# Final sums of batches 1 to 4 beside the expert blocks, with a check of the counts on the chip and a branch that repeats them

## The chip, the core and the metric

The kernel runs on one core of one Trainium2 chip. TensorE (PE in the profile; PEld is its weight load) multiplies matrices, VectorE (DVE) and ScalarE (ACT) work elementwise, GpSimd (POOL) issues here the indirect DMAs, and SyncE (SP) issues plain ones. Each engine runs its own instruction stream in order; semaphores tie them together. The metric is the device time of one execution in microseconds (us), as a median of runs. The kernel before took 1891.41 us (three runs, 1890.63 to 1898.66).

## What is computed

Eight batches of 512 tokens with 256 features (4096 tokens in all) go through four residual steps:

```python
x = x + attn_a(layernorm(x), ...)   # projection, silu, a recurrence with decay 0.9, projection
x = x + ffn(layernorm(x), ...)      # mixture of experts
x = x + attn_b(layernorm(x), ...)   # causal attention, 16 heads of 16
x = x + ffn(layernorm(x), ...)      # the mixture once more, same weights
```

The mixture picks 4 of 16 experts for each token (two of four groups, then the best four in them), runs a gated network of width 256 in each picked expert, weights the four results, and adds a shared network that every token passes:

```python
topk_idx, tw = _route(x, router_w, bias)
routed = sum over the picked experts e of  tw[e] * ((silu(x @ gate_w[e]) * (x @ up_w[e])) @ down_w[e])
sh = silu(x @ sh_gate_w) * (x @ sh_up_w) @ sh_down_w
return routed + sh
```

## The kernel before, in words

The work has two pairs of stages: a stretch over the eight batches (first the recurrence, then the attention), and after each stretch a routed stage, in which the picked experts run. Weights of all experts stay in on-chip memory (`w_all`).

*In a stretch*, batch by batch, the tokens are normalised and routed. `choices` finds each token's four experts and its place among the rows of each expert: `row` is a running count of the rows of each expert, carried from batch to batch in `counts[i]` (L610 to L613), so after batch b it says how many rows each of the 16 experts has up to there, plus the fixed start of the expert's region. One indirect DMA of GpSimd per 128 tokens and choice (L648) writes the normalised tokens, their weights and their token numbers into `xg`, sorted by expert. `shared_experts` computes the shared network. Two arrays in device memory, `parts[i][0]` and `parts[i][1]`, hold the result of the mixture in two halves: the residual rows are stored into the first (`part<-x`), the shared network's into the second (`part<-ys_m`), and what the experts make is later added into both.

`blocks` (L662) then makes a table of blocks. A block is 128 rows of one expert. The order of the blocks is by their number within an expert first and by expert second: the first block of all experts, then the second of all that have one, and so on. Since rows are sorted in the order of batches, early batches lie in early blocks. The number of blocks of each expert is `nb`. There are at most 143 blocks (`NBLK`), and 136 (`LIKELY`) are always run.

*In a routed stage* (`routed`, L748), a block n passes five steps: `load` (SP reads the 128 rows from `xg`), `fetch` (ACT and DVE copy the expert's gate and up weights to a fixed place, L787), `turn` (PE transposes the rows, L794, ACT copies them, L795), `up` (PE, sixteen matmuls, L805, then ACT and two DVE multiplications, L813 to L815), and `down` (PE, four matmuls, L833, ACT scales, L841). `down` ends with an indirect DMA of GpSimd, the scatter (L842), that adds the rows of the block into one of the two halves of `parts[i]`: even blocks into the first, odd ones into the second. `run` interleaves the steps of neighbouring blocks: the load is two blocks ahead of `up`, `fetch` and `turn` one ahead, `down` two behind. The tiles of the rows come from a set of nine buffers (tag `kb4`), so that a load for block n uses the buffer whose last reader was the scatter of block n-9. The copied weights share six buffers (tag `col`).

Ahead of the 136 blocks stands a branch (L875): all five engines load the number of blocks, compare it with 136, and take either an arm that runs blocks 136 to 142 or an arm that only brings the semaphores to the counts which the first one would have left.

`beside` is a dictionary from a block number to functions: after `down(n - 2)` the functions of key n - 1 are called. In the second routed stage it holds the final sums of batches 0 and 1. The final sum of a batch reads its rows of both halves of `parts[1]`, adds them on VectorE (L1289) and stores them to the output. `DONE` says after how many blocks a batch is complete whatever the routing: 64 for batch 0, 128 for batch 1, 143 for the others. So batch 0 is loaded at block 64 and added and stored at block 69, batch 1 at 128 and 133. These loads and stores are issued by GpSimd (L1282, L1292), into the buffers of `xpool` (three) and of the attention's values (two). The addition is pinned behind what was traced before it on VectorE. The other six batches are summed after the last block: SP loads one half, ACT the other, and they store in turn; their tiles use the nine `kb4` buffers.

The order of instructions on an engine is settled when the program is built, by a scheduler that works through the traced instructions by priority and readiness and places a semaphore wait wherever data, a buffer or an order in a DRAM tensor asks for one: a load from a half of `parts[1]` waits for all scatters into that half that come before it, and a scatter after it waits for the load. Scatters into the same half follow each other. The two arms of a branch are scheduled as a unit.

Of the kernel before, what the change touches and what calls it, by code (L numbers as in the profile page):

```python
# [10 lines left out]
FP = mybir.dt.float32  # L11
AF = mybir.ActivationFunctionType
ALU = mybir.AluOpType
AX = mybir.AxisListType

P = 128
B, T, D = 8, 512, 256
NT = T // P
# [8 lines left out]
E, F = 16, 256  # L27
# [19 lines left out]
NJ = NTOK // BLK  # L47
DONE = [min(E * (b + 1) * NT, NBLK) for b in range(B)]
CAND = NJ * E // P
WEXP = 2 * KD * F + KF * D  # L50
I32 = mybir.dt.int32
# [3 lines left out]
KB, COLS = 9, 6  # L55
HALVED = 1597463007.0
SENT = 8
EARLY = 2
PICKS = 5
ES, QK = 6, 6  # L60
ATT_SCALE = 0.25
# [9 lines left out]
def tile_hybrid_block(  # L71
# [22 lines left out]
    nc = tc.nc  # L94
# [3 lines left out]
    work = ctx.enter_context(tc.tile_pool(name="work", bufs=2))  # L98
    small = ctx.enter_context(tc.tile_pool(name="small", bufs=2))
# [86 lines left out]
    def load_expert(e: int):  # L186
# [13 lines left out]
        out=before,  # L200
        in_=before,
# [17 lines left out]
    def load_attention_weights():  # L219
# [16 lines left out]
        out=causal, in_=causal, compare_op=ALU.is_ge, fill=0.0, base=0, pattern=[[0, 2], [1, P]], channel_multiplier=-1  # L236
# [6 lines left out]
        out=tri, in_=tri, compare_op=ALU.is_gt, fill=0.0, base=0, pattern=[[1, P]], channel_multiplier=-1  # L243
# [6 lines left out]
    region = const.tile([P, E], FP, name="region")  # L250
# [252 lines left out]
        return sel  # L503

    counts = [region, region]

    class Route:

# [44 lines left out]
    def choices(i: int, b: int, tag: str, held):  # L553
# [57 lines left out]
        for t in range(NT):  # L611
            nc.vector.tensor_add(row[:, t + 1, :], pr[:, 1, t, :], row[:, t, :])
        counts[i] = row[:, NT, :]  # L613
        where = small.tile([P, NT, E], FP, tag="where", name=f"where_{tag}", bufs=1)
        nc.vector.tensor_add(where, pr[:, 0], row[:, 0:NT, :])
        yield
# [45 lines left out]
    def blocks(i: int, table):  # L662
# [67 lines left out]
        for which in range(2):  # L730
# [7 lines left out]
            else:  # L738
# [3 lines left out]
                    behind_all, number[0:1, :], total[0:1, :], float(E * REG), ALU.is_ge, ALU.mult  # L742
                )
                nc.vector.tensor_add(lines[:, 1, :], pl, behind_all)
        table += [lines[:, 0, :], lines[:, 1, :], expert, many]
        yield

    def routed(i: int, table, beside):  # L748

        weight_at, row_at, expert, many = table  # L750
        ACT, DVE = mybir.EngineType.Activation, mybir.EngineType.DVE
        PE, SP = mybir.EngineType.PE, mybir.EngineType.SP
        held = {}
# [520 lines left out]

    with banks_of(big=4, misc=2, y=2):

        def sum_of(b: int, homes):

            both = []
            for j, queue in enumerate((nc.sync, nc.scalar) if b >= EARLY else (nc.gpsimd, nc.gpsimd)):  # L1280
                both.append(homes(j))
                queue.dma_start(  # L1282
                    out=both[j],
                    in_=parts[1][j][b * T : (b + 1) * T, :].rearrange("(p t) d -> p (t d)", p=P),
                )
            return both

        def add_up(b: int, both):
            added = nc.vector.tensor_add(both[0], both[0], both[1])  # L1289
            if b < EARLY:  # L1290
                tc.keep_in_program_order(added)
            ((nc.sync, nc.scalar)[b % 2] if b >= EARLY else nc.gpsimd).dma_start(  # L1292
                out=out[b].rearrange("(p t) d -> p (t d)", p=P), in_=both[0]
            )

        sums = {}

        def early(b: int):
            def homes(j: int):
                tile = xpool.tile([P, NT, D], FP, tag="x", name=f"sum_{b}_0") if j == 0 else values(f"sum_{b}_1")  # L1300
                return tile.rearrange("p t d -> p (t d)") if j == 0 else tile[:, 0 : NT * D]

            return {
                DONE[b]: [lambda: sums.update({b: sum_of(b, homes)})],
                DONE[b] + 5: [lambda: add_up(b, sums.pop(b))],
            }

        routed(1, table, {**early(0), **early(1)})
        for b in range(EARLY, B):
            add_up(  # L1310
                b,
                sum_of(b, lambda j: work.tile([P, NT * D], FP, tag="kb4", name=f"sum_{b}_{j}", bufs=KB)),
            )


# [40 lines left out]
```

## Time and profile before

The profile is of one execution of 1906.2 us, with a span of 1904.0 us from the first to the last instruction and a mean granted TensorE clock of 0.945.

| | start us | end us |
|---|---|---|
| first routed stage, first to last transposes | 407.2 | 796 |
| second routed stage, first transposes on PE | 1471.5 | |
| last matmul of the stage | | 1865.0 |
| last scatter issued by GpSimd | 1872.7 | |
| first loads of the closing sums, SP and ACT | 1874.3 | 1876.6 |
| first and last closing addition | 1883.2 | 1900.1 |
| end of the span | | 1904.0 |

Over the span PE is busy 1723.5 us (91%), DVE 1085.4 (57%), ACT 797.3 (42%) and POOL 764.1 (40%). In the profile, a line of a timeline gives the start, the duration, the engine, the line of the kernel, the operation, the tiles it writes and reads, and in square brackets how long the engine was idle before it and what ended that wait. Neighbouring equal instructions are merged (x4), and the duration is then that of the whole group. A sequencer's own instructions carry a q (SPq, ACTq): their duration is that of issuing a DMA, not of the transfer.

### The profile page before, as it was taken

The numbers are of one execution on the slowest core, as the hardware profiler recorded it, in microseconds if no ns is written. First come the engines' busy times: TensorE is split into PE (matmuls) and PEld (weight loads), VectorE is DVE, ScalarE is ACT, GpSimd is POOL, SyncE is SP. The second block draws the span as 40 slices with busy tenths as digits, with TensorE's granted clock in tenths as the row PEclk, the third lists the DMA queues.
The fourth block names the chain that finished last, engine by engine and source line by source line (L and its number), as shares of the span: only waits on it lengthen the run. The fifth ranks groups of instructions, "written<-read, shape, count | busy, mean of one in ns | idle before, by whom it ended". The sixth has DMA issues, their size and how long they took to land. (4 is left out here: it accounts for less than half of the span.)

```text
span 1904.0 us, 32586 instructions
## 1 busy us (share of the span) xinstructions
PE 1723.5 (91%) x10640; PEld 1277.8 (67%) x10640; DVE 1085.4 (57%) x3378; ACT 797.3 (42%) x1628; POOL 764.1 (40%) x665
## 2 busy tenths in 40 slices
PE   5899999969999999899988989889886999999991
PEld 3566656559999999834444535445354999999991
DVE  6866666525555655657746556456543555555552
ACT  2322222125555555455534444344411555555550
POOL 4254544345555555500223031230333455565552
PEclk9899999889999999999989989899888999999996
DMA  4443321435555655511112111021144455565557
GB/s 157 155 140 122 125 75 72 145 105 95 96 98 103 106 96 96 93 39 34 41 40 81 45 48 57 36 86 45 65 146 138 80 96 97 95 130 95 96 101 240
DMA packets 149995, 181.35 MB, mean 95 GB/s; under 512 B 16096, under 2 KB 136960, under 8 KB 149824
## 3 DMA queue, kind: packets, MB, share of 16 engines
q0 software_dynamic: 53136, 76.81, 22.4%
q1 hardware_dynamic: 94320, 96.12, 16.6%
q10 hardware_dynamic: 2368, 6.29, 0.8%
q8 instruction: 89, 1.46, 0.3%
q14 instruction: 82, 0.67, 0.1%
HBM read 81.62 MB, written 97.53 MB: 94 GB/s over the span
## 5 line engine op out<-in xcount | busy, mean ns | idle before, releaser
L842 POOL DMA_INDIRECT part<-rows x272 | 425.9, 1566 | 367.9 <-ACT rows L841 317.5
L648 POOL DMA_INDIRECT xg<-sorted_m,slots_m x256 | 257.3, 1005 | 268.4 <-DVE sorted_m L638 133.8
L805 PEld LDWEIGHTS ph<-rows,gate 128*128 128x128 f32 x2176 | 285.8, 193 | 15.2 <-ACT rows L795 1.1
L805 PE MATMUL ph<-rows,gate 128*128 128x128 f32 x2176 | 289.0, 277 | 0.6 <-ACT rows L795 0.6
L805 PE MATMUL ph<-rows,up 128*128 128x128 f32 x2176 | 289.1, 277 | 0.0
L833 PE MATMUL pyr<-w_all,rows 128*128 x1088 | 282.1, 382 | 4.4 <-DVE rows L815 3.4
L805 PEld LDWEIGHTS ph<-rows,up 128*128 128x128 f32 x2176 | 266.5, 193 | 0.0
L813 ACT ACTIVATE rows<-ph 128x256 f32<-128x256 f32 x272 | 104.2, 383 | 330.2 <-PE ph L805 326.2
L814 DVE TENSOR_TENSOR rows<-ph,rows 128x256 f32<-128x256 f32 x272 | 115.4, 424 | 201.9 <-ACT rows L813 165.1
L833 PEld LDWEIGHTS pyr<-w_all,rows 128*128 128x128 f32 x1088 | 186.0, 192 | 19.0 <-issue 3.2
L787 ACT COPY gate<-w_all 128x512 f32 x272 | 170.0, 626 | 14.2 <-DVE up L787 2.0
L1039 ACT ACTIVATE w_all<-ps_a 128x1024 f32<-128x1024 f32 x128 | 124.8, 1021 | 111.6 <-PE ps_a L1028 63.6
L787 DVE COPY up<-w_all 128x512 f32 x272 | 117.9, 434 | 48.0 <-ACTq L875 25.2
L1028 PE MATMUL ps_a<-w_all 32*128 32x512 f32 (+3 forms) x1024 | 129.8, 488 | 15.0 <-issue 7.3
L922 PE MATMUL pd_m<-sd_sb,act_m 128*128 128x256 f32 x512 | 133.3, 409 | 5.4 <-DVE act_m L913 3.6
L841 ACT ACTIVATE rows<-pyr,gain 128x256 f32<-128x256 f32 x272 | 128.4, 472 | 20.1 <-PE pyr L833 18.6
L894 PE MATMUL pg_m<-xT_m,su_sb 128*128 128x512 f32 x256 | 132.0, 640 | 4.9 <-DVE x L426 3.9
L794 PE MATMUL pt<-ident,rows 128*128 128x128 f32 x544 | 105.0, 275 | 33.2 <-DMA rows<-xg 33.2
L894 PE MATMUL pg_m<-xT_m,sg_sb 128*128 128x512 f32 x256 | 127.4, 621 | 0.3 <-issue 0.3
L922 PEld LDWEIGHTS pd_m<-sd_sb,act_m 128*128 128x128 f32 x512 | 104.1, 207 | 30.5 <-issue 6.1
L815 DVE TENSOR_TENSOR rows<-ph,rows 128x256 f32<-128x256 f32 x272 | 115.2, 424 | 8.2
L818 DVE SCALAR_TENSOR_TENSOR gain<-rows,expert_b 128x4 f32<-128x4 f32 x272 | 60.4, 222 | 97.8 <-ACT rows L841 85.0
(207 smaller groups left out, 2199.6 us busy)
## 6 DMA issues: line engine op xcount, KB each, us to landing
rows<-xg SPq DMA_DIRECT2D x272, 136.0 KB
part<-x SPq DMA_DIRECT2D x16, 512.0 KB
part<-ys_m SPq DMA_DIRECT2D x16, 512.0 KB
w_all<-in_L_ffn_gate_w_dram SPq DMA_DIRECT2D x24, 256.0 KB
w_all<-in_L_ffn_up_w_dram SPq DMA_DIRECT2D x24, 256.0 KB
w_all<-in_L_ffn_down_w_dram SPq DMA_DIRECT2D x24, 256.0 KB
xg<-zeros SPq DMA_DIRECT2D x34, 136.0 KB
part<-rows POOLq DMA_INDIRECT x272
```

The source lines that it names most:

```text
L648: nc.gpsimd.indirect_dma_start(out=xg[i], out_offset=bass.IndirectOffsetOnAxis(ap=slots[:, at : at + 1], axis=0), in_=rows[:, t, :], in_of ...
L787: copy(here, w_all[:, bass.ds(held[n][0] + half * KD * F, KD * F)])
L805: nc.tensor.matmul(ph[:, s, f * P : (f + 1) * P], lhsT=both[s][:, k * F + f * P : k * F + (f + 1) * P], rhs=rows[:, ROW + k * P : ROW + (k ...
L814: nc.vector.tensor_mul(act, ph[:, 0, :], act)
L815: nc.vector.tensor_mul(act, ph[:, 1, :], act)
L833: nc.tensor.matmul(py, lhsT=act[:, f * P : (f + 1) * P], rhs=w_all[:, bass.ds(w + 2 * KD * F + f * D, D)], start=(f == 0), stop=(f == KF - 1),
L841: nc.scalar.mul(rows[:, 0:D], py, gain[:, TK : TK + 1])
L842: nc.gpsimd.indirect_dma_start(out=parts[i][n % 2], out_offset=bass.IndirectOffsetOnAxis(ap=rows[:, D + 2 * TK : D + 2 * TK + 1].bitcast(U ...
L894: nc.tensor.matmul(dst, lhsT=w[:, k, f * P : (f + 1) * P], rhs=xnT[:, k, :], start=(k == 0), stop=(k == KD - 1),)
L922: nc.tensor.matmul(py[:, j, :], lhsT=acts[n][:, f, t * P : (t + 1) * P], rhs=shared[n][3][:, f, :], start=(n == 0 and f == 0), stop=(n == ...
L1028: nc.tensor.matmul(ps[j // 2][:, j % 2, col : col + n], lhsT=k_sb[w][r, o, c * P : (c + 1) * P], rhs=q_sb[r, o, c * P : T], start=True, st ...
L1039: nc.scalar.activation(es[two], ps[two][:, :, 0:cols], AF.Exp, scale=ATT_SCALE)
```

## The change

The dictionary `SUMMED` takes the place of `EARLY` and `DONE` for the final sums: batches 0 to 4 are summed beside the blocks, loaded at blocks 64, 76, 88, 110 and 127 and added and stored five blocks later, all loads and stores issued by GpSimd. Only batches 5 to 7 are always summed after the last block.

Blocks 76, 88, 110 and 127 are not late enough for every possible routing. So `choices` keeps the counts after each of the batches 0 to 4 (`upto`), and `check`, beside blocks 14, 18, 22 and 26, works out from them how many blocks of the order the batch needs: the rows of each expert up to this batch, in blocks; the largest of these over the experts; the sum over the experts of the smaller of that and the expert's number of blocks. It marks the batch in `lates` if that is more than `SUMMED` allows. `checked`, beside block 40, adds up the marks. After the last block SP, ACT and VectorE load the sum of marks into registers; if it is above zero, a branch repeats the sums of batches 0 to 4.

```diff
--- before.py
+++ after.py
@@ -55,7 +55,9 @@
 KB, COLS = 9, 6
 HALVED = 1597463007.0
 SENT = 8
-EARLY = 2
+
+
+SUMMED = {0: DONE[0], 1: 76, 2: 88, 3: 110, 4: 127}
 PICKS = 5
 ES, QK = 6, 6
 ATT_SCALE = 0.25
@@ -503,6 +505,7 @@
         return sel
 
     counts = [region, region]
+    upto = {}
 
     class Route:
 
@@ -611,6 +614,9 @@
         for t in range(NT):
             nc.vector.tensor_add(row[:, t + 1, :], pr[:, 1, t, :], row[:, t, :])
         counts[i] = row[:, NT, :]
+        if i == 1 and b in SUMMED:
+            upto[b] = small.tile([1, E], FP, tag=f"upto_{b}", name=f"upto_{b}", bufs=1)
+            nc.vector.tensor_copy(upto[b], row[0:1, NT, :])
         where = small.tile([P, NT, E], FP, tag="where", name=f"where_{tag}", bufs=1)
         nc.vector.tensor_add(where, pr[:, 0], row[:, 0:NT, :])
         yield
@@ -742,12 +748,12 @@
                     behind_all, number[0:1, :], total[0:1, :], float(E * REG), ALU.is_ge, ALU.mult
                 )
                 nc.vector.tensor_add(lines[:, 1, :], pl, behind_all)
-        table += [lines[:, 0, :], lines[:, 1, :], expert, many]
+        table += [lines[:, 0, :], lines[:, 1, :], expert, many, nb]
         yield
 
     def routed(i: int, table, beside):
 
-        weight_at, row_at, expert, many = table
+        weight_at, row_at, expert, many, _ = table
         ACT, DVE = mybir.EngineType.Activation, mybir.EngineType.DVE
         PE, SP = mybir.EngineType.PE, mybir.EngineType.SP
         held = {}
@@ -1274,10 +1280,12 @@
 
     with banks_of(big=4, misc=2, y=2):
 
-        def sum_of(b: int, homes):
+        beside = (nc.gpsimd, nc.gpsimd)
+
+        def sum_of(b: int, homes, queues=(nc.sync, nc.scalar)):
 
             both = []
-            for j, queue in enumerate((nc.sync, nc.scalar) if b >= EARLY else (nc.gpsimd, nc.gpsimd)):
+            for j, queue in enumerate(queues):
                 both.append(homes(j))
                 queue.dma_start(
                     out=both[j],
@@ -1285,13 +1293,11 @@
                 )
             return both
 
-        def add_up(b: int, both):
+        def add_up(b: int, both, queues=(nc.sync, nc.scalar)):
             added = nc.vector.tensor_add(both[0], both[0], both[1])
-            if b < EARLY:
+            if queues is beside:
                 tc.keep_in_program_order(added)
-            ((nc.sync, nc.scalar)[b % 2] if b >= EARLY else nc.gpsimd).dma_start(
-                out=out[b].rearrange("(p t) d -> p (t d)", p=P), in_=both[0]
-            )
+            queues[b % 2].dma_start(out=out[b].rearrange("(p t) d -> p (t d)", p=P), in_=both[0])
 
         sums = {}
 
@@ -1301,16 +1307,62 @@
                 return tile.rearrange("p t d -> p (t d)") if j == 0 else tile[:, 0 : NT * D]
 
             return {
-                DONE[b]: [lambda: sums.update({b: sum_of(b, homes)})],
-                DONE[b] + 5: [lambda: add_up(b, sums.pop(b))],
+                SUMMED[b]: [lambda: sums.update({b: sum_of(b, homes, beside)})],
+                SUMMED[b] + 5: [lambda: add_up(b, sums.pop(b), beside)],
             }
 
-        routed(1, table, {**early(0), **early(1)})
-        for b in range(EARLY, B):
-            add_up(
-                b,
-                sum_of(b, lambda j: work.tile([P, NT * D], FP, tag="kb4", name=f"sum_{b}_{j}", bufs=KB)),
+        late = small.tile([1, 1], I32, tag="late", name="late", bufs=1)
+        lates = small.tile([1, len(SUMMED)], FP, tag="lates", name="lates", bufs=1)
+        nc.gpsimd.memset(lates, 0.0)
+
+        def check(b: int):
+
+
+            nb = table[4]
+            one = small.tile([1, E + 2], FP, tag="one", name=f"one_{b}", bufs=1)
+            n, most, done = one[:, 0:E], one[:, E : E + 1], one[:, E + 1 : E + 2]
+            nc.vector.tensor_sub(n, upto[b], region[0:1, :])
+            shape = [1, E, NJ]
+            more = work.tile(shape, FP, tag="col", name=f"above_{b}", bufs=COLS)
+            nc.vector.tensor_tensor(
+                more, n.unsqueeze(2).to_broadcast(shape), steps[0:1, :].unsqueeze(1).to_broadcast(shape), ALU.is_gt
             )
+            nc.vector.tensor_reduce(n, more, AX.X, ALU.add)
+            nc.vector.tensor_reduce(most, n, AX.X, ALU.max)
+            nc.vector.tensor_scalar(n, nb[0:1, :], most, None, ALU.min)
+            nc.vector.tensor_reduce(done, n, AX.X, ALU.add)
+            nc.vector.tensor_scalar(lates[:, b : b + 1], done, float(SUMMED[b]), None, ALU.is_gt)
+
+        def checked():
+            any_late = small.tile([1, 1], FP, tag="any_late", name="any_late", bufs=1)
+            nc.vector.tensor_reduce(any_late, lates, AX.X, ALU.add)
+            nc.vector.tensor_copy(late, any_late)
+
+        plan = {}
+        for b in SUMMED:
+            for at, do in early(b).items():
+                plan.setdefault(at, []).extend(do)
+            if SUMMED[b] < DONE[b]:
+                plan.setdefault(10 + 4 * b, []).append(lambda b=b: check(b))
+        plan.setdefault(40, []).append(checked)
+        routed(1, table, plan)
+
+        def at_the_end(b: int):
+            add_up(b, sum_of(b, lambda j: work.tile([P, NT * D], FP, tag="kb4", name=f"sum_{b}_{j}", bufs=KB)))
+
+        _, (again,) = nc.values_load_multi_w_load_instructions(
+            late,
+            engines=[mybir.EngineType.SP, mybir.EngineType.Activation, mybir.EngineType.DVE],
+            min_val=0,
+            max_val=len(SUMMED),
+            skip_runtime_bounds_check_because="a count of batches",
+        )
+        with tc.If(again > 0):
+            for b in SUMMED:
+                at_the_end(b)
+        for b in range(B):
+            if b not in SUMMED:
+                at_the_end(b)
 
 
 # ---- launch: one core; inputs and outputs as the reference has them ----
```

## The prediction

> **What bounds the kernel now.** I read the windows by stage first, then the chain that ended last, then the timeline of the end, and last the timeline around the two early sums that the kernel already has. In the windows (the window's start and end and its length, busy time by engine with instruction counts, clock, DMA share, GB/s) the last routed stage, its end without PE, and the closing sums stand apart:
>
> ```profile
> 1472.00:1865.00 393.00, 392.50 (x2991) 377.12 (x2990) 219.81 (x678) 214.84 (x541) 210.74 (x138) 0.99 0.59 100
> 1865.00:1876.60 11.60, 0.00 (x0) 0.00 (x0) 0.00 (x0) 0.47 (x1) 6.59 (x5) 0.67 0.64 99
> 1876.60:1904.00 27.40, 0.00 (x0) 0.00 (x0) 7.35 (x6) 0.00 (x0) 0.00 (x0) 0.50 0.85 338
> ```
>
> For 393 us PE is the bound (392.5 busy); VectorE is at 56%. Then the scatters drain for 11.6 us, and for 27.4 us only DMAs and six additions run. The timeline of the end shows what the 27.4 us are:
>
> ```profile
> 1872.68 1.55 POOL L842 DMA_INDIRECT part<-rows  x1 [0.78 <-issue]
> 1874.29 1.90 SPq L1282 DMA_DIRECT2D sum<-part  x4
> 1876.59 1.80 ACTq L1282 DMA_DIRECT2D sum<-part  x4
> 1883.16 5.14 DVE L1289 TENSOR_TENSOR sum<-sum,sum 128x1024 f32<-128x1024 f32 x4 [19.45 <-DMA sum<-part]
> ...
> 1898.91 1.23 DVE L1289 TENSOR_TENSOR sum<-sum,sum 128x1024 f32<-128x1024 f32 x1 [2.70 <-DMA sum<-part]
> 1900.17 0.34 ACTq L1292 DMA_DIRECT2D out_dram<-sum  x1
> ```
>
> Eight loads go out at once, eight buffers of the nine; the last four loads wait for buffers until 1884.9 to 1888.7. Six batches move 6 x 3 x 0.524 = 9.44 MB; where the traffic is full it runs at about 415 GB/s.
>
> The price of a sum beside the blocks is seen at block 64, on POOL (start, duration, idle before it):
>
> ```profile
> 1660.59 1.56 POOL L842 DMA_INDIRECT part<-rows  x1 [1.31 <-ACT rows L841]
> 1664.73 0.60 POOL L1282 DMA_DIRECT2D sum<-part  x1 [2.58 <-DMA part<-rows]
> 1665.63 1.59 POOL L842 DMA_INDIRECT part<-rows  x1 [0.30 <-issue]
> 1670.10 0.58 POOL L1282 DMA_DIRECT2D sum<-part  x1 [2.88 <-DMA part<-rows]
> 1670.99 1.58 POOL L842 DMA_INDIRECT part<-rows  x1 [0.30 <-ACT rows L795]
> 1675.00 2.03 POOL L842 DMA_INDIRECT part<-rows  x1 [2.42 <-DMA part<-rows]
> ```
>
> A load of a sum waits until the last scatter into its half has landed, and the next scatter into that half waits for the load. PE takes a block every 2.87 us, so the three scatters after 1660.59 were due at 1663.46, 1666.33 and 1669.20; they came 2.2, 4.7 and 5.8 us late. The scatter of block 74, at 1696.78, is still 1.8 late, that of block 80, at 1712.22, is on time: 4.0 us are recovered in the first nine blocks, 5.8 in fifteen, 0.39 per block. The addition holds VectorE meanwhile, and PE follows:
>
> ```profile
> 1674.36 1.23 DVE L1289 TENSOR_TENSOR sum<-sum,sum 128x1024 f32<-128x1024 f32 x1 [2.13 <-DMA sum<-part]
> 1675.51 0.42 DVE L787 COPY up<-w_all 128x512 f32 x1
> 1677.74 1.06 PE L805 MATMUL ph<-rows,up 128*128 128x128 f32 x8
> ```
>
> VectorE stood 2.13 us for the loads; the weight copy behind it ended at 1675.93, 1.8 us before its matmuls (5.1 us is usual). PE kept its 2.87 us throughout. So one such sum is free for PE, with 1.8 us in hand.
>
> **The change, part by part.** *The closing sums, 6 to 3.* Removed: 6 of 12 loads, 3 of 6 additions, 3 of 6 stores, 4.72 MB. By rate alone, 4.72 MB / 415 GB/s = 11.4 us. Followed through: SP issues three loads from 1874.3 and ACT three from 1876.6, all at once, since six buffers are free at once. Before, eight loads (4.19 MB) were in by about 1886.9, 11.4 us after data began near 1875.5, or 368 GB/s; six (3.15 MB) take 8.5 us, to 1884.0. The last addition (1.23) ends at 1885.3, and from the end of the last addition to the end of the span is 1904.0 - 1900.14 = 3.9 us: 1889.2. If the first two stores (1.05 MB) get in the way of it all, 2.5 us more: 1891.7. Gain 12.3 to 14.8; I take 13.5, the middle, since the first store can start only when most loads are in.
>
> *Three sums more beside the blocks, and batch 1 moved from 128 to 76.* Sums now begin at 64, 76, 88, 110 and 127, and each adds its 5.8 us of lateness to what is left. At 76 the last undisturbed scatter is that of block 74, 1.8 us late: 7.6 at the peak. Nine blocks later 3.6 are left as 88 comes: 9.4. VectorE is in program order, so its wait for the loads grows by the same amounts: at 76 from 2.13 to 3.9, which uses up the 1.8 us in hand, stall 0; at 88 to 5.7, a PE stall of 1.8 us. This stall takes 1.8 from the lateness too; nineteen blocks at 0.39 take the other 7.4, so 110 starts with about 0.2, and 127 with 0.6. The rows of later blocks: a rows load waits for the scatter nine blocks back. Its lead over the transposes falls from 10.8 to 4.95 us after block 64 (issued 1679.42, turned 1684.37); less 1.8 it is 3.1 at 76, and less 3.6 but plus the stall 3.1 at 88. A rows load took 2.2 us in the chain (1469.98), so no second stall. Sum: +1.8. Low end 0 (the stall is put on the wait of a single event); high end 6.7, if the recovery is half as fast (under the rivals).
>
> POOL issues nine DMAs more, beside the blocks: they are inside the 5.8 us. SP and ACT lose nine transfers at the end and gain none beside the blocks.
>
> The last of these sums, at 127 rather than 128, leaves the final scatter where it was: 0.6 us residue less one block of recovery, 0.4. Cost 0.2.
>
> [...] POOL's issue of a sum load took 0.60 us against 0.33 on SP and 0.39 on ACT, small beside the 5.8 us of waits, and those waits come from the halves being shared with the scatters. [...]
>
> *The checks.* Four times eight VectorE instructions, at blocks 14, 18, 22 and 26. By the rows with the same free size: subtraction 0.15 (L679), comparison over 512 0.68 (L682), reduction of 512 0.69 (L686), three reductions or minima of 16 at 0.16 (L688), one last compare 0.13 (L690): 2.1 us each, 8.5 in all. The cover: copies are there 4 to 5 us before their matmuls in these blocks, and VectorE has 1.2 us free per block, so 2.1 us are made up in two blocks. Cost 0; at most 8.5, if all of it falls in PE's way. Five copies of 1x16 in the attention stage (0.13 to 0.17 each, 0.8 in all) and the clearing of five numbers on POOL: 0, at most 1.
>
> *The branch.* Register loads on SP, ACT and DVE (1.06 each by SP's at L765), a compare, the count-keeping arm. The nearest rows are those of the branch ahead of the blocks:
>
> ```profile
> L875 PEldq COMPARE_BRANCH  x2: 400/1980/3561, 389.0 to 1451.7; - x2
> L875 DVEq COMPARE_BRANCH  x2: 62/67/72, 390.5 to 1452.4; - x2
> L875 ACTq COMPARE_BRANCH  x2: 45/45/45, 401.2 to 1465.3; - x2
> L875 SPq COMPARE_BRANCH  x2: 45/48/50, 402.4 to 1466.7; - x2
> ```
>
> On the three engines it is under 0.1 us, and ACT's next copy came 1.6 us after its branch (1465.3 to 1466.92). At the end SP is free from 1848.2 and needed at 1874.3, ACT from 1865.5 to 1876.6, DVE from 1863.7 to 1883: 2.7 us hide in 11. Cost 0. Upper end: that earlier branch stands in a PE gap of 16.5 us (1455.05 to 1471.53). [...]
>
> Whether the repeats run is a matter of data. The reference's routing on its inputs gives the counts that the check compares: 48, 64, 80 and 111 for batches 1 to 4, against 76, 88, 110 and 127. It is not taken.
>
> **Sum.** -13.5 + 1.8 + 0.2 = -11.5 us. The profiled execution took 1906.2 us (span 1904.0), so 1894.7; it is 14.8 above the median of the runs, 1891.4, and the same difference there gives 1879.9.
>
> **Rivals.** *The lateness stays.* If only half is recovered between sums, 76 starts with 3.8 and PE stalls 2.0, 88 with 5.6 and 3.8, the other two 0.9, and the last scatter is 1 later: gain 13.5 - 6.7 - 1 = 5.8, 1885.6. For it: five sums share one POOL queue, and the recovery was seen only with 60 free blocks behind. Against: 0.39 per block is read from two halves of one curve. *The branch holds (ends slower).* If the three engines can enter it only when the last scatter has landed (1876.6), and it then costs the 16.5 us of the earlier gap: 1896.4. It decides above 11.5 us. Against: that gap ends with a wait for rows, which end-of-stage scatters feed. With PE's 3.56 alone it is 1883.5. *The checks get in the way*, since nothing pins their place: 1888.4 at worst. *The change does not do what it says*: a count is over its bound, all five repeat, and eight batches close: 12.6 MB, 3.15 more than before, 7.6 us, with the stalls and buffer waits about 10: 1901.
>
> **How the numbers follow.** Likeliest case 0.62, its own range 1876 to 1883. Lateness 0.18, around 1886; checks or another order 0.09; the branch 0.08; repeats 0.03. The range 1875 to 1892 leaves out most of the branch and the repeats above, and 15.5 us and more of gain below. Half a per cent, 9.5 us, is about what a measurement tells from no change: faster, below 1882, is most of the first case and a little of the others, 0.62; same 0.27; slower 0.11, from the repeats and the far ends of branch, lateness and checks.
>
> **What would show it.** After the last scatter: three loads on SP and three on ACT, three additions, and about 13 us from the last scatter's landing to the end of the span. POOL's lateness near 7.6 after 76 and 9.4 after 88; a PE step above 2.87 only near blocks 94 to 97. Wrong: PE steps lost at several sums, the first closing load well after 1877 on a scatter that has landed, or additions of batches 0 to 4 at the end.

## The result and the profile after

After the change the kernel took 1893.59 us (median of 20 runs, 1884.37 to 1903.56), the kernel before 1893.04 us beside it (20 runs, 1880.73 to 1901.83). The ratio is 1.0004, with a 95% interval of 0.9985 to 1.0023: no difference that can be measured. The forecast, 1879.9 us and a range up to 1892, was wrong.

The profiled execution of the changed kernel took 1893.99 us with a span of 1891.9, against 1906.2 and 1904.0 before. Of that difference of 12 us, 10 aren't the change: the second routed stage, up to which hardly anything differs, began at 1471.5 us in the one profile and at 1461.4 in the other, and another profile of the unchanged kernel (the first experiment) has it at 1461.0. So all that follows is measured from the first transposes of the second routed stage. The windows of the kernel after (start and end, length, busy time of PE, PEld, DVE, ACT, POOL with instruction counts, clock, DMA share, GB/s), cut as before the change at the last matmul and the last scatter's issue:

```profile
1461.40:1864.00 402.60, 396.48 (x2992) 379.22 (x2992) 229.73 (x712) 216.30 (x540) 217.79 (x147) 0.99 0.61 110
1864.00:1872.60 8.60, 0.00 (x1) 0.00 (x0) 0.00 (x0) 0.47 (x1) 5.88 (x5) 0.70 0.49 59
1872.60:1891.90 19.30, 0.00 (x0) 0.00 (x0) 3.60 (x3) 0.00 (x0) 1.53 (x1) 0.50 0.76 258
```

The blocks take 402.6 us where they took 393.4 (from the first transposes at 1471.5 to 1865.0). From the last matmul to the end of the span it is 27.9 us where it was 39.1. The two nearly cancel: +9.3 and -11.2, together -1.9 us, inside the interval of the ratio (-2.8 to +4.4 us). The end went as the change has it, in the timeline of the kernel after:

```profile
1872.59 1.54 POOL L848 DMA_INDIRECT part<-rows  x1 [0.56 <-issue]
1874.25 1.32 SPq L1290 DMA_DIRECT2D sum<-part  x3
1876.47 2.07 ACTq L1290 DMA_DIRECT2D sum<-part  x3
1884.17 3.72 DVE L1297 TENSOR_TENSOR sum<-sum,sum 128x1024 f32<-128x1024 f32 x3 [21.43 <-DMA sum<-part]
```

Three loads on each queue, three additions, no sum of batches 0 to 4: the branch was not taken. From the last scatter's issue to the end of the span it is now 19.3 us; it was 31.3.

Where the blocks lost 9 us is seen at the sum of batch 1, loaded at block 76 and added at 81. POOL's timeline of the kernel after:

```profile
1687.76 1.57 POOL L848 DMA_INDIRECT part<-rows  x1 [0.32 <-issue]
1691.83 0.59 POOL L1290 DMA_DIRECT2D sum<-part  x1 [2.49 <-DMA part<-rows]
1692.72 1.58 POOL L848 DMA_INDIRECT part<-rows  x1 [0.30 <-ACT rows L847]
1697.45 0.59 POOL L1290 DMA_DIRECT2D sum<-part  x1 [3.15 <-PE pt L800]
1698.35 1.57 POOL L848 DMA_INDIRECT part<-rows  x1 [0.30 <-ACT gate L793]
1703.44 2.02 POOL L848 DMA_INDIRECT part<-rows  x1 [3.52 <-DMA part<-rows]
```

The three scatters after 1687.76 were due at 1690.63, 1693.50 and 1696.37; they came 2.1, 4.9 and 7.1 us later than that. A scatter stands usually 10.6 us behind the transposes of its block. Measured against that, the scatter of block 74 was already 3.6 us late (forecast: 1.8), and that of block 77 was 10.6 late (forecast: 7.6). What follows on VectorE and PE, in the timeline of the kernel after:

```profile
1702.82 1.23 DVE L1297 TENSOR_TENSOR sum<-sum,sum 128x1024 f32<-128x1024 f32 x1 [6.91 <-DMA sum<-part]
1703.96 0.42 DVE L793 COPY up<-w_all 128x512 f32 x1
1704.43 2.08 PE L811 MATMUL ph<-rows,up 128*128 128x128 f32 x8 [2.85 <-DVE up L793]
1708.43 1.92 PE L811 MATMUL ph<-rows,gate 128*128 128x128 f32 x8
```

VectorE stood 6.91 us at the addition, with the copy of the next block's weights behind it in order. PE waited 2.85 us for that copy. And then its matmuls ran at half speed: eight of them took 2.08 and 1.92 us where 1.06 and 1.05 are usual. The windows of the kernel after behind the wait show it in the clock (the sixth value behind the length):

```profile
1701.50:1703.60 2.10, 0.08 (x1) 0.00 (x0) 0.79 (x1) 0.00 (x0) 0.16 (x1) 1.00 0.28 47
1703.60:1710.40 6.80, 5.97 (x24) 5.61 (x25) 4.88 (x17) 1.75 (x4) 5.93 (x4) 0.50 0.59 117
1710.40:1712.00 1.60, 1.60 (x13) 1.55 (x13) 0.61 (x2) 0.62 (x3) 1.38 (x1) 0.98 1.06 253
```

The granted clock, 1.00 from 1690 to 1703.6, is 0.50 for 6.8 us, up to 1710.4. It falls during the wait, 2.0 us after PE went idle at 1701.58, and stays at half for 6.0 us after the wait has ended. The two blocks there were 6.0 us longer than 2.87 each: 2.85 of waiting and 3.2 of slow matmuls (half of those 6.0 us would be 3.0). From the twentieth block on, the blocks lost 10.0 us; the stage as a whole is only 9.3 longer than before, since the profile before is 0.7 slower in the first twenty. PE's waits in the kernel after, from 1600 us on (total us, times, longest), come from the same additions or from rows that arrive late:

```profile
PE ph L811 <- DVE up L793: 3.6, 2, 2.9
PE pt L800 <- DMA rows<-xg: 0.9, 2, 0.7
PE pyr L839 <- DVE rows L821: 0.9, 1, 0.9
```

The second wait of the first row is 0.78 us, at the sum of batch 3. The third row is the sum of batch 4: VectorE stood 5.28 us at its addition, and the multiplications behind it (L820, L821) came late for PE at 1858.5. So the sums of batches 1, 3 and 4 stop PE through VectorE, and late rows take 0.9 us.

### The profile page after: what moved, and what is told of

Read it like the earlier page. It is cut to its first block, busy times and chain, and to the rows that moved or that the text cites. A ratio compares the mean times of both kernels' runs of the same rounds, so it can differ in the third digit from the quotient of the medians.

```text
span 1891.9 us, 32623 instructions
## 1 busy us (share of the span) xinstructions
PE 1725.1 (91%) x10640; PEld 1276.7 (67%) x10640; DVE 1091.4 (58%) x3413; ACT 799.0 (42%) x1628; POOL 772.9 (41%) x675
## 5 line engine op out<-in xcount | busy, mean ns | idle before, releaser
L820 DVE TENSOR_TENSOR rows<-ph,rows 128x256 f32<-128x256 f32 x272 | 115.2, 424 | 181.5 <-ACT rows L819 157.0
L928 PE MATMUL pd_m<-sd_sb,act_m 128*128 128x256 f32 x512 | 129.0, 398 | 8.7 <-DVE act_m L919 5.0
L1034 PE MATMUL ps_a<-w_all 32*128 32x512 f32 (+3 forms) x1024 | 125.0, 482 | 12.0 <-ACT w_all L1045 6.6
L928 PEld LDWEIGHTS pd_m<-sd_sb,act_m 128*128 128x128 f32 x512 | 100.0, 199 | 33.3 <-issue 8.8
L821 DVE TENSOR_TENSOR rows<-ph,rows 128x256 f32<-128x256 f32 x272 | 115.1, 423 | 8.2 <-DVE rows L820 0.2
```

Source lines behind the costliest of these rows:

```text
L820: nc.vector.tensor_mul(act, ph[:, 0, :], act)
L821: nc.vector.tensor_mul(act, ph[:, 1, :], act)
L928: nc.tensor.matmul(py[:, j, :], lhsT=acts[n][:, f, t * P : (t + 1) * P], rhs=shared[n][3][:, f, :], start=(n == 0 and f == 0), stop=(n == ...
L1034: nc.tensor.matmul(ps[j // 2][:, j % 2, col : col + n], lhsT=k_sb[w][r, o, c * P : (c + 1) * P], rhs=q_sb[r, o, c * P : T], start=True, st ...
```

## The experiments

Two theories to begin with. A: VectorE, in program order, is held at the additions, because they stand only five blocks behind their loads; PE waits for the weight copies behind them. B: the scatters' lateness itself reaches PE, through buffers and rows that come late. A third, C: the checks' instructions on VectorE get in the way. "Stage" is the time from the first transposes of the second routed stage to its last matmul, "end" from there to the end of the span, in the profiled execution; "stall" is what the blocks from the twentieth on took over 2.868 us each. Two of the three groups of runs were made at a higher granted clock, 0.97 to 0.98 in place of 0.95, where the kernel before took 1781.39 and 1778.35 us: times are compared only with the kernel before beside them, and stage and end can be compared throughout, since the clock in the stage is 0.99 in both.

| kernel | stage | end | together | stall |
|---|---|---|---|---|
| before | 393.4 | 39.1 | 432.5 | 0.0 |
| before, again | 394.1 | 39.0 | 433.1 | 0.0 |
| after | 402.7 | 27.9 | 430.6 | 10.0 |
| additions nine blocks behind the loads | 394.1 | 28.0 | 422.2 | 0.0 |
| no checks, no branch | 402.6 | 26.5 | 429.1 | 8.9 |
| no sums of batches 1 to 4 | 393.7 | 21.2 | 414.9 | 0.0 |
| batch 4 with the closing sums | 401.7 | 28.4 | 430.1 | 8.2 |
| sums every 16 blocks | 399.2 | 26.4 | 425.6 | 5.2 |
| loads of the sums on SP | 395.7 | 22.7 | 418.4 | 1.7 |
| sums from 40, additions nine behind | 393.9 | 21.8 | 415.7 | 0.2 |
| the same, loads on SP | 394.3 | 21.8 | 416.2 | 0.2 |
| repeats taken | 399.2 | 50.5 | 449.6 | 5.7 |

**The kernel before, again.** No edit.

> The kernel before, profiled a second time, to see what repeats. Measured from the first transposes of the second routed stage: 393.4 us to the end of the last matmul, 39.0 more to the end of the span, 432.4 in all in the first profile. All theories expect these to repeat within 1 us, with no PE step above 2.87 us after block 19, while the time at which the stage begins (1471.5) may move by 10 us with the clock of the stages before it.

One run took 1896.23 us. Stage and end agree with the first profile to 0.7 and 0.1 us, so differences of 2 us in them can be read where PE doesn't stall. Where it does, the same blocks vary more: the plan of the kernel after lost 10.0, 8.9 and 5.7 us in three profiles of the table (after, no checks, repeats taken). The stage began at 1461.01.

**The additions four blocks later.** Nothing but the distance from the loads to the addition, and with it to the store of the sum, is changed:

```diff
-                SUMMED[b] + 5: [lambda: add_up(b, sums.pop(b), beside)],
+                SUMMED[b] + 9: [lambda: add_up(b, sums.pop(b), beside)],
```

> The changed kernel with the addition and the store nine blocks after the loads in place of five; loads, checks and branch as they are. Theory A (the 12 us won at the end are lost because VectorE, in program order, stands at the addition for up to 6.9 us and holds PE): the waits of the additions fall below 1 us, no PE wait on a weight copy or on the second multiplication is left, and the block stage falls from 402.7 us to between 393.5 and 397, what is left being rows that come late; from the start of the stage to the end of the span 421 to 425 instead of 430.5. Theory B (the late scatters, through the rows buffers, or the traffic itself cost it): the stage stays at 400 or more and the whole at 428 or more. Theory C (checks or branch): the same as B.

The stage is back at 394.1, with no stall at all. The whole took 1885.12 us in one run, beside 1889.37 for the kernel before; single runs of the kernel before differ by more than that (1889.37 and 1896.23). At the sum of batch 1 in the timeline of this kernel:

```profile
1690.41 0.59 POOL L1290 DMA_DIRECT2D sum<-part  x1 [2.43 <-DMA part<-rows]
...
1695.94 0.59 POOL L1290 DMA_DIRECT2D sum<-part  x1 [3.05 <-PE pyr L839]
...
1708.02 1.22 DVE L1297 TENSOR_TENSOR sum<-sum,sum 128x1024 f32<-128x1024 f32 x1
```

POOL's waits for the scatters are as before the edit (2.43 and 3.05 against 2.49 and 3.15 us), and the lateness peaks at 7.3, 8.1, 7.6 and 9.3 us at the four sums. But the addition no longer waits (no bracket), and none of the five does. So lateness of 7 to 9 us is harmless here by itself: it is the wait of VectorE that carries it to PE. That speaks for A and against B at these sizes. (At batch 1 the lateness is smaller too, 7.3 against 10.6; at the other three it is 1.0 less to 0.9 more than in the kernel after.) The later addition delays the last sum as well (last scatter 10.2 us behind the last matmul, against 8.6), without moving the end.

**No checks and no branch.** The counts' copies, the checks, the register loads and the branch are removed; the sums stay where they are. What the kernel leaves out is only the test of completeness.

```diff
-            if SUMMED[b] < DONE[b]:
-                plan.setdefault(10 + 4 * b, []).append(lambda b=b: check(b))
-        plan.setdefault(40, []).append(checked)
...
-        _, (again,) = nc.values_load_multi_w_load_instructions(
...
-        with tc.If(again > 0):
-            for b in SUMMED:
-                at_the_end(b)
```

> The changed kernel without the copies of the counts, the checks and the branch (nothing guards the sums then). A and B: stage 402 to 403, end 27 to 28, 430 in all, as with them. C: at least 3 us less in all.

Stage 402.6 against 402.7 and a stall of 8.9 against 10.0; the end is 1.4 us shorter. C falls: the checks cost the blocks nothing that shows beside the variation of the stall. In the kernel after, the compare and branch took 50 ns on SP (at 1852.2), 63 on VectorE (1863.0) and 45 on ACT (1864.4). All three are through 8 us ahead of the last scatter's issue at 1872.6.

**No sums of batches 1 to 4.** This measures the floor: the sums of these batches are left out, their output is not written; batch 0 is still summed beside the blocks.

```diff
-            for at, do in early(b).items():
+            for at, do in (early(b) if b == 0 else {}).items():
```

> The changed kernel with the sums of batches 1 to 4 left out (their outputs are not written; the sum of batch 0, the checks, the branch and the three closing sums stay). A and B: the stage is back at 393.4 us and the end stays at 27 to 28, 421 in all, so that the sums themselves cost about 9 us. C: the stage or the end is longer than these by several us.

Stage 393.7, no stall. New is the end: 21.2 us, 6.7 less than in the kernel after with the same three closing sums. The last scatter goes out 3.5 us behind the last matmul, against 8.6 in the kernel after and 7.7 before. So a sum at 127 or 128 holds the last scatters up by 4 to 5 us, and this was already paid before the change. It is not the change's loss, but it is there to be won.

**Batch 4 at the end.** Is it worth having the sum at 127 at all?

```diff
-SUMMED = {0: DONE[0], 1: 76, 2: 88, 3: 110, 4: 127}
+SUMMED = {0: DONE[0], 1: 76, 2: 88, 3: 110}
```

> The changed kernel with batch 4 summed after the last block: four sums beside the blocks, four at the end. By the run that left out the sums, the last scatter was issued 3.5 us after the last matmul in place of 8.6, since no sum at 127 held GpSimd up; one closing sum more is 1.57 MB at about 415 GB/s, 3.8 us. So the end should be 24 to 26 us, 2 to 4 less than with batch 4 at 127, and the stall of 1.2 us after 127 goes too: whole 425 to 428. If the sum at 127 is worth its place, the end is 29 us or more.

The last scatter came at 3.5 us, as in the kernel without these sums. But with four closing sums the end from there on takes 24.9 us in place of 17.7 to 19.3, so the whole end is 28.4 against 27.9: nothing won. A fourth closing sum cost about 5.6 to 7.2 us, more than the 3.8 that the rate of the closing loads gives (1.57 MB at 415 GB/s). Why was not followed up. The stall at the sum of batch 1 came again, with the half clock. Timeline of this kernel:

```profile
1587.46 1.22 DVE L1297 TENSOR_TENSOR sum<-sum,sum 128x1024 f32<-128x1024 f32 x1 [7.48 <-DMA sum<-part]
1589.08 2.07 PE L811 MATMUL ph<-rows,up 128*128 128x128 f32 x8 [3.43 <-DVE up L793]
```

**Sums every 16 blocks.** If lateness adds up because batches 1 and 2 follow after 12 blocks, a wider spacing should take the stall away:

```diff
-SUMMED = {0: DONE[0], 1: 76, 2: 88, 3: 110, 4: 127}
+SUMMED = {0: DONE[0], 1: 80, 2: 96, 3: 112, 4: 128}
```

> The changed kernel with the five sums 16 blocks apart (64, 80, 96, 112, 128), additions still five blocks after the loads. If the stalls came from lateness that one sum leaves to the next (3.5 us left at block 74, 14.2 less the usual 10.6, and 7 more from the sum itself): the lateness peaks at about 18 after each sum in place of 21, VectorE waits 2.5 to 4 us per addition, and PE loses at most 1 us at 80, 96 and 112; stage 394 to 396, whole 422 to 425. If each sum on its own is dear, wherever it stands: stage 400 or more.

One run took 1768.47 us, beside 1781.39 for the kernel before. The stage is 399.2: the stall fell to 5.2, not to 1; neither of the two expectations met it. VectorE's waits are 3.2, 3.4, 3.8, 4.2 and 1.8 us (2.7, 6.9, 3.5, 4.8 and 5.3 in the kernel after) and PE no longer waits for the copies behind them. But it waits for rows, in the waits of this kernel:

```profile
PE pt L800 <- DMA rows<-xg: 4.0, 4, 2.0
```

Here B shows, but lateness alone doesn't explain it: its peaks are 6 to 8 us, and with the additions four blocks later 9.3 us brought no wait for rows. What these four have in common is the store of a sum, which POOL issues 0.9 to 1.5 us ahead of the load of the rows. The longest wait, in the timeline of this kernel:

```profile
1690.58 1.24 POOL L1300 DMA_DIRECT2D out_dram<-sum  x1
1692.05 0.33 SPq L785 DMA_DIRECT2D rows<-xg  x1
1697.12 0.41 PE L800 MATMUL pt<-ident,rows 128*128 128x128 f32 x2 [1.97 <-DMA rows<-xg]
```

From the issue of such a load to the transposes that waited for it are 5.0, 4.4, 4.0 and 5.1 us. With the additions four blocks later the store stands elsewhere, and the rows issued latest, 2.96 us ahead of their transposes, were in time. So here late scatters and the store's traffic together make rows late; how much each does, no run shows. Spacing alone is half a remedy.

**Loads of the sums on SP.** The loads of the sums leave POOL's queue for SP's; their stores stay on POOL.

```diff
-                SUMMED[b]: [lambda: sums.update({b: sum_of(b, homes, beside)})],
+                SUMMED[b]: [lambda: sums.update({b: sum_of(b, homes, (nc.sync, nc.sync))})],
```

> The changed kernel with the ten loads beside the blocks issued by SP in place of GpSimd; the stores stay on GpSimd. If plain loads do better off the GpSimd queue: the lateness of the scatters peaks under 15 (usual 10.6), no PE stall is left, stage under 396, whole under 424. If what costs is the order in the halves (a load waits for the last scatter, the next scatter for the load), the lateness still peaks at 16 or more, and the loads of rows, now queued on SP behind those waits, come late too: lead under 3 us, stage 400 or more.

One run took 1762.31 us, beside 1781.39 for the kernel before. The timeline of this kernel at batch 1:

```profile
1575.43 1.55 POOL L848 DMA_INDIRECT part<-rows  x1 [3.73 <-DMA rows<-xg]
...
1580.24 1.92 POOL L848 DMA_INDIRECT part<-rows  x1 [3.25 <-DMA rows<-xg]
```

Two scatters wait 3.73 and 3.25 us for a transfer of SP's queue. The bracket names a load of rows, but that queue now carries the loads of the sums too, and which of them it was can't be told from the line. What is gone is POOL's own standing at the issue of a load (2.49 and 3.15 us in the kernel after). The lateness peaks at 4.2, 5.4, 7.6, 3.9 and 4.3 us instead of 6.4 to 10.6, VectorE's waits sum to 6.5 us instead of 23.2, and the last scatter is only 4.7 behind the last matmul. That rows come late, as the second expectation has it, is seen once: PE waited 1.4 us, at block 98, whose load was issued 0.9 us behind the store of a sum. Together 418.4 against 430.6, 14.1 below the kernel before. Of the two expectations the first had stage and whole right (under 396 and 424), but two of the five peaks are over its lateness of 15 - 10.6 = 4.4 us, and one PE wait was left.

**Earlier sums and later additions.** The wider spacing and the later additions put together, with what the counts allow: the inputs need 48, 64, 80 and 111 blocks for batches 1 to 4, and for batch 0 block 40 is tried, which the same check now covers.

```diff
-SUMMED = {0: DONE[0], 1: 76, 2: 88, 3: 110, 4: 127}
+SUMMED = {0: 40, 1: 58, 2: 76, 3: 94, 4: 112}
...
-                SUMMED[b] + 5: [lambda: add_up(b, sums.pop(b), beside)],
+                SUMMED[b] + 9: [lambda: add_up(b, sums.pop(b), beside)],
```

> The five sums 18 blocks apart from block 40 on (40, 58, 76, 94, 112), additions nine blocks after the loads, batch 0 checked too. By theory A and the run without the sums: lateness back at 10.6 before each sum, no PE step above 2.87 us, last scatter 3.5 us after the last matmul, end 21 to 22 us, whole 415 to 416, some 17 us under the kernel before: ratio about 0.991. If lateness or traffic cost PE something that the additions only hid: stage above 396 and a ratio of 0.994 or more.

1760.93 us (4 runs, 1759.90 to 1762.65) against 1781.39 (7 runs): 0.9893, interval 0.9876 to 0.9909. It is faster than the kernel before; the changed kernel, which had 1.0004 of that one, wasn't run beside it. The windows of this kernel, the blocks and the end:

```profile
1342.30:1736.30 394.00, 393.43 (x2992) 377.32 (x2992) 232.87 (x719) 215.72 (x541) 220.97 (x149) 0.99 0.61 113
1736.30:1758.00 21.70, 0.00 (x0) 0.00 (x0) 3.61 (x3) 0.47 (x1) 3.67 (x3) 0.59 0.72 236
```

The five sums cost nothing: stage and end are those of the kernel that leaves four of them out, within 0.2 and 0.6 us. The branch was not taken. With 24 blocks free behind the last sum, the last scatter goes out 3.4 us behind the last matmul.

**The additions four blocks later, timed.** The same kernel as in the first of the experiments on A, with enough runs for an interval:

```diff
-                SUMMED[b] + 5: [lambda: add_up(b, sums.pop(b), beside)],
+                SUMMED[b] + 9: [lambda: add_up(b, sums.pop(b), beside)],
```

> The changed kernel with additions nine blocks after the loads once more, timed against the kernel before. By the profiles its second routed stage with the end is 422.2 us against 432.5 and 433.1, so theory A expects 10 us less than before, a ratio of 0.994 to 0.995, where the change itself had 1.0004. If the profiles of the stage do not say what happens in unprofiled runs, the ratio stays within 0.998 to 1.002.

1773.08 us (11 runs, 1766.76 to 1776.95) against 1778.35 (16 runs): 0.9965, interval 0.9952 to 0.9978. The gain is real, but 5 us and not the 9 that stage and end give (423.4 against 432.5). The profiled execution, 1767.67, was one of its fastest, 5.4 us under the median of these runs. The stages of the other executions aren't on record, so where the other 4 us go stays open. This profile has a stall of 1.1 us, at blocks 97 and 98, where rows came late; their shortest lead over the transposes was 2.3 us. No store is near, and the lateness there, 9.6 us, is the largest of the runs with later additions: at that size it reaches PE by itself.

**Repeats taken.** The check is turned round, so that the branch runs the five sums again (as in the prediction's last rival):

```diff
-            nc.vector.tensor_scalar(lates[:, b : b + 1], done, float(SUMMED[b]), None, ALU.is_gt)
+            nc.vector.tensor_scalar(lates[:, b : b + 1], done, float(SUMMED[b]), None, ALU.is_le)
```

> The changed kernel with the comparison of the check turned round, so that the marks are set and the branch repeats the sums of batches 0 to 4. The prediction put eight closing sums in place of three at about 10 us over the kernel before with six. Measured from the last matmul to the end: 28 us with three sums, about 39 with six; five more sums at 3.8 us each give 47 us. If the branch itself costs several us when it is taken (code to be fetched, the arm as a unit), 52 or more.

One run took 1795.73 us, 17 above the kernel before (1778.35). Its timeline at the end:

```profile
1753.81 1.42 SPq L1290 DMA_DIRECT2D sum<-part  x3
...
1777.88 1.32 SPq L1290 DMA_DIRECT2D sum<-part  x3
```

The first line has the first three of the ten loads of the repeats, the second those of batches 5 to 7 on SP. These go out only when the repeats' stores have been issued: 24 us after the first ones. The last addition ends at 1789.7. The two groups come one after the other, not as one stream of eight. This profile is of use in another way: up to the end its program is that of the kernel after but for one comparison, and its addition at batch 1 waited 4.57 us, not 6.91, PE 0.52 us, and the two groups of eight matmuls behind that wait took 1.16 and 1.05 us, not 2.08 and 1.92. Lateness was 2.4 us at block 74 and 8.3 at block 77, in place of 3.6 and 10.6. The stall was 5.7, not 10.0. So the same stage loses a varying amount; of the 4.3 us between these two, 3.2 are the slow matmuls behind the longer wait.

**Earlier sums, later additions, loads on SP.** Both remedies together:

```diff
-SUMMED = {0: DONE[0], 1: 76, 2: 88, 3: 110, 4: 127}
+SUMMED = {0: 40, 1: 58, 2: 76, 3: 94, 4: 112}
...
-                SUMMED[b]: [lambda: sums.update({b: sum_of(b, homes, beside)})],
-                SUMMED[b] + 5: [lambda: add_up(b, sums.pop(b), beside)],
+                SUMMED[b]: [lambda: sums.update({b: sum_of(b, homes, (nc.sync, nc.sync))})],
+                SUMMED[b] + 9: [lambda: add_up(b, sums.pop(b), beside)],
```

> Sums at 40, 58, 76, 94 and 112, additions nine blocks later, loads issued by SP. If SP's queue only shortens the lateness, there is nothing left to win over the run with GpSimd's loads at these blocks: stage 394, end 21 to 22, ratio 0.988 to 0.991. If SP's waits hold up rows: stage above 395.

1762.42 us (5 runs, 1759.54 to 1763.31) against 1778.35 (16 runs): 0.9911, interval 0.9897 to 0.9925. Stage 394.3, end 21.8: no better than without the loads on SP. With room between the sums and later additions nothing is left that the loads on SP could remove.

## Why the prediction was wrong

By its steps, in us:

| step | forecast | measured |
|---|---|---|
| closing sums, 6 to 3 | -13.5 (-12.3 to -14.8) | -12.0 |
| sums beside the blocks | +1.8 (0 to 6.7) | +9.3 |
| last scatter | +0.2 | +0.9 |
| checks, branch | 0 | 0 to 1.4 |
| together | -11.5 | -1.9 |

(The measured rows are rounded; the checks are contained in the others. +9.3 is the longer stage, 10.0 the stall from the twentieth block on.)

The step that failed is the one on the three early sums, at 76: VectorE's wait grows from 2.13 to 3.9 us, "which uses up the 1.8 us in hand, stall 0". The wait was 6.91, and it cost 6.0 us at that place alone; the total was 10.0 where 1.8 was forecast. The step has four faults, by size:

- *The price of a stall.* It was taken as the length of the wait. PE's clock fell to half in a wait of 2.85 us, and 3.2 us more went there. The prediction never asked what a wait does to the matmuls behind it.
- *The starting lateness.* 3.6 us was left at block 74, not 1.8. The two profiles of the kernel before have 1.2 and 1.8 there; the six with the changed plan that load batch 0 by POOL at 64 and add it at 69, the kernel after among them, have 2.4 to 4.8; the two that add it at 73 have 1.5. In the kernel after, the scatter behind the store of batch 0 came 4.3 us after the one before it, in the kernel before 2.75. Why isn't settled.
- *What the sum adds.* 7.0 us at batch 1, where the sum of batch 0 had shown 5.8 and showed 6.4 now.
- *No margin.* The forecast put the stall exactly on the edge, with 1.8 us in hand and 1.8 used up. At such an edge every error to one side is a stall, and none to the other is a gain: 0 is the best case, not the middle.

The size itself varies: the same blocks in the run with the repeats lost 5.7 us, still inside the step's upper end of 6.7 and three times its value.

What was right: that an early sum delays the scatters, VectorE's program order as the path from there to PE, and the 1.8 us in hand. By the forecast PE stalls when VectorE waits longer than 2.13 + 1.8 = 3.9 us; measured are 6.91 - 2.85 = 4.1 at batch 1, 4.83 - 0.78 = 4.05 at batch 3, and 4.57 - 0.52 = 4.05 in the run with the repeats. The run with the additions four blocks later shows this path: the scatters are late still, the wait is gone, and the stage returns to 394.1. The places "only near blocks 94 to 97" were wrong: the largest stall was at 84 and 85. The closing sums gained 1.5 us less than the value taken and 0.3 less than its lower bound. The forecast let one addition of 1.23 us follow the last load; measured, the three stood back to back behind the loads, from 1884.17 for 3.72 us, which is 2.5 us more. Checks and branch cost the blocks nothing, as forecast; the end is 1.4 us shorter without them, in one profile of each. The repeats were not taken.

Of the rivals, "the lateness stays" was the nearest: half the recovery, 6.7 us of stall, 1885.6. Its path is right, lateness left over at 76 that stops PE through VectorE. Its reason isn't shown: with the additions four blocks later the lateness fell from 7.3 at block 77 to 2.8 at 86, 0.50 us per block against 0.39 in the forecast, and in the kernel after, up to the stall, from 10.6 at 77 to 8.6 at 83, 0.33 and not half. Its largest stall, 3.8 at 88, was none either (VectorE waited 3.49 there, under the 3.9 in hand). That its total came nearest is in good part luck. The branch and the checks fell. Where the repeats were made to run, the end took 50.5 us; that rival had 10 us over the kernel before, and 17 were measured, since the two groups of closing sums don't overlap.

The range, to 1892, held the stall's upper end (6.7) as one rival alone, at 1885.6, and no stall beyond that. With the measured sum, -1.9 on 1891.4 gives 1889.5, still inside the range; the changed kernel's median lies 4.1 us above that. Of these 1.6 are the kernel before, which took 1893.04 in this comparison; for the other 2.5, the interval of the ratio reaches from -2.8 to +4.4 us and holds -1.9. So it was the size of the stall that took away the gain, and the last 1.6 us out of the range are no more than the measurement leaves open.

## What to carry to other kernels

With the additions nine blocks behind their loads, where VectorE, which stands in order between them and PE, had room, the blocks lost 0.0 to 1.1 us in four profiles; with five blocks they lost 10.0 in the kernel after. So give an in-order engine between such work and the bound engine room: place what waits for a DMA (here an addition) so far behind its load that it does not wait even when the load comes late. Here four blocks more, 11 us, won back in the profiles all of the 9 us that the move had cost the blocks; the timed runs kept 5 us of gain over the kernel before. And put such work where the blocks behind it can recover, not at the end of the stage: the last sum at 112 instead of 127 brought the last scatter 5 us forward.

## What the runs showed of the hardware

The longest waits of PE in the blocks, nearly 3 us and more, cost clearly more than their length. With a wait of 2.85 us, in the kernel after, the granted clock was 0.50 for 6.8 us, 6.0 of them behind the wait, and groups of eight matmuls took 2.08 and 1.92 us in place of 1.06 and 1.05; after waits of 2.97 and 3.43 us, in the kernel without checks and in the one with batch 4 at the end, the first group took 1.85 and 2.07. The two blocks at the wait were 1.9 to 3.2 us longer than by the wait alone, about half of the time at half clock behind it: 3.4 us without checks, 6.0 in the other two. The length of the wait alone did not say when the clock fell: 2.0 us into the wait in the kernel after, 2.6 into it with batch 4 at the end, and without checks only 0.3 us behind its end. The last two are worked out from the clock in windows: with batch 4 at the end 0.89 from 1585.6 to 1589.0, 0.50 up to 1594.0 and 0.73 up to 1596.0; without checks 1.00 from 1702.8 to 1705.8, 0.56 up to 1708.0 and 0.63 up to 1710.0. A wait of 1.97 us, for rows in the kernel with sums every 16 blocks, cost 2.1 us and no clock, in the windows of that kernel around it (the clock is 1.00 in both, ahead of the DMA share):

```profile
1695.00:1697.10 2.10, 0.16 (x2) 0.01 (x1) 0.02 (x1) 0.38 (x1) 1.42 (x1) 1.00 0.72 136
1697.10:1699.10 2.00, 1.98 (x14) 1.89 (x15) 1.51 (x5) 1.34 (x3) 0.79 (x1) 1.00 0.50 71
```

By the windows the half clock came in stretches of about 6.8 us in the kernel after and with batch 4 at the end, and of about 3.4 without checks. Of these waits the shortest that the fall came with was that of 2.85 us, and PE had been idle for 2.0 of them when the clock fell. What a wait between 1.97 and 2.85 us does, no run here shows, and none shows what makes the clock fall or what sets how long it stays down.
